# A neighbourhood-quantile layer: small writes behind the vector engine's operations, shorter sort operations, and a last pair finished batch by batch

## The chip, the cores and the metric

The kernel runs on one core of a Trainium2 chip. A core has five engines with a queue each: TensorE (PE in the profile, its weight loads PEld), VectorE (DVE), ScalarE (ACT), GpSimd (POOL) and SyncE (SP). The engines run their own instructions in order and wait for one another through semaphores. The metric is the time of one execution on the device in microseconds; lower is better.

## What is computed

For 16 graphs of 1024 nodes with 64 channels, every node aggregates its neighbours' features by quantiles and passes the result through a small two-layer network. The reference, cut to what matters:

```python
h = relu(layernorm(x))
neigh = (adj > 0) & ~eye
rank = cumsum(neigh) - neigh                    # place of a neighbour in its row
skip = where(nb > 10, (nb + 1) // 2, 1)         # nb: number of neighbours
rem = neigh & (skip > 1) & (rank % skip == skip - 1) & mask
nd = (adj with rem and rem.T dropped) > 0
s = sort(where(nd, h, inf), over the neighbours)        # per node and channel
agg = sum(w * quantile(s, tau) for tau, w in ((.25, .25), (.5, .5), (.75, .25)))
y = (relu((h + agg) @ W1 + b1) @ W2 + b2) * mask
return x + y
```

## The kernel before

The 16 graphs (batches) are worked in 8 pairs. For one batch, `prepare` does what precedes the sort: `load` turns the adjacency rows into signs and transposes them, `drop` (L979, tile `rem`) finds the edges that are dropped, `keep` and `order` sort the nodes by their number of neighbours (L1047, tile `perm`, is the one-hot matrix of that order), and `collect` writes for every node the list of its neighbours (tile `idx`). The features lie in a table in DRAM (`gtab`).

The sorted nodes form 8 tiles of 128, and the tiles form four classes of like degree: tile 0 with 13 slots, tiles 1 to 3 with 11, tiles 4 and 5 with 9, tiles 6 and 7 with 7. For each slot, tile and batch one indirect DMA on POOL's queue (`gather` in `fetch`, L1250) fetches the rows of 128 neighbours into a tile `g` (`g0`, `g1`, `g4`, `g6` by class): 126 gathers for a pair, 1008 in all. The 32 nodes of highest degree of each batch are finished apart, in groups of 8 batches (tiles `gg`, `fetch_group`, `aggregate_group`), and `scatter` (L1498) writes their rows of the output by two indirect DMAs for a group.

`sort` runs a fixed network over the slots of one class. A step of the network takes `n` comparisons of lines at once: one DVE operation writes the minima (L1288), one the maxima (L1289); steps that need one side alone are L1285. A line holds the class's tiles, both batches and 64 channels: 384 numbers in a partition for the 11-slot class, 256 for the 9- and 7-slot classes, 128 for the 13-slot class and the group. The operations are therefore up to 768 wide. At the end the slots are multiplied with the quantiles' weights (L1296) and added up by PE (L1298, one fp32 matmul with the identity for each slot). `let_go` puts a one-element write into a tile `pause` (L1268) behind an operation whenever some 0.8 us of sort operations have gone by without one; `arrange` keeps those writes as `tails` of their operation.

`aggregate` does this for both halves of a pair's tiles (half 0: classes 13 and 11; half 1: classes 9 and 7), both batches together, and `terms` (L1312, L1314) splits the sum into three bf16 terms, tile `o`. `mlp` then, for one batch and each 512 nodes, builds a one-hot matrix (`one_hot`, L1373, tile `at_p`), brings the nodes back into their order with it (L1392 `high`, L1397 `low`, 8 matmuls each), and applies the two layers (L1410, L1411, L1414, `output`).

The order of each engine's queue isn't the order of the code: `arrange` takes all instructions, gives each a cost (`Step.cost`), simulates five engines and fixes the order in which each engine runs its own. `settle` ties instructions into a run that must stay in order. The gathers stand in a queue of their own that `weave` empties at an even rate beside the other work. In the program's order the last steps are: aggregation of the last pair, its four one-hot matrices, `mlp` for batches 14 and 15, then the scatter of the last group and a check value (`worst`, `flag`), which decides whether a general version of the layer has to run.

Of the kernel before, what the change touches and what calls it, by code (L numbers as in the profile page):

```python
# [43 lines left out]
P = 128  # L44
N = 1024
C = 64
# [42 lines left out]
SPREAD = 160  # L89

# [510 lines left out]
class Step:  # L601
# [11 lines left out]
    def cost(self):  # L613
        sides = self.writes + self.reads
        most = max([u.count for u in sides] or [1])
        if self.engine == "PE":
            n, lines = self.writes[0].count, self.writes[0].lines
            if any(u.size == 4 for u in self.reads):
                busy = 223 if n <= 64 else max(428, n / 0.6)
            else:  # L620
                busy = max(25, n / 2.4 + 3)
            return busy * 1.15 / (4 if lines[1] - lines[0] <= 32 else 2 if lines[1] - lines[0] <= 64 else 1), 200
# [17 lines left out]
def arrange(tc, runs, tails=()):  # L640

    steps, found, number = [], {}, {}
    for ins in list(tc.nc.cur_bb.bb.instructions):
        if type(ins).__name__.startswith("BassTile"):
            continue
        if ins.name in tails:
            at = found[tails[ins.name]]
            at.tail.append(ins)
            number[ins.name] = len(number)
            at.busy += Step(ins, 0).busy  # L650
            found[ins.name] = at
            continue
        found[ins.name] = Step(ins, len(steps))
        steps.append(found[ins.name])
# [82 lines left out]

    for steps in sequence.values():
        alike = iter(sorted((i for s in steps for i in s.tail), key=lambda i: number[i.name]))
        line = [i for s in steps for i in (s.ins, *(next(alike) for _ in s.tail))]  # L740
# [8 lines left out]
def list_layer(  # L749
# [25 lines left out]
    def settle(run):  # L775

        runs.append([ins.ins.name for ins in run])
        for ins, then in zip(run, run[1:]):
# [6 lines left out]
            tc.info.no_tile_sem_insts.add(ins.ins.name)  # L785
        if len(run) > 1:
            tc.declare_fence(run[-1].ins, group=f"run{len(runs)}")

# [168 lines left out]
    def drop(b):  # L957
# [5 lines left out]
        for t in range(NT):  # L963
# [15 lines left out]
            nc.vector.tensor_scalar(rem[:, t], dist, 1.0, half[:, t:t + 1], OP.add, OP.is_equal)  # L979
# [32 lines left out]
    def order(b):  # L1012
# [30 lines left out]
        nc.vector.scalar_tensor_tensor(mask2[:, b], place_f, float(FEW), mask[:, b], OP.is_ge, OP.mult)  # L1043
        yield 1.2
        perm = wk.tile([P, NT, N], BF16, name="perm", tag="wide", bufs=1)
        for t in range(NT):
            nc.vector.tensor_scalar(perm[:, t], turned, place_f[:, t:t + 1], None, OP.is_equal)  # L1047
# [173 lines left out]
    tails = {}  # L1221
# [3 lines left out]

    queue = deque()
# [11 lines left out]
    def fetch(m, classes=CLASSES, halves=(0, 1)):  # L1238

        for tiles, slots in classes:  # L1240
# [8 lines left out]
            def gather(h, slot, k, at, tiles=tiles, lo=lo):  # L1249
                return nc.gpsimd.indirect_dma_start(  # L1250
                    out=gathered[m, tiles][:, slot, k - lo, h], out_offset=None, in_=tables[2 * m + h][0],
                    in_offset=bass.IndirectOffsetOnAxis(ap=lists[2 * m + h][:, at:at + 1], axis=0),
                    element_offset=tables[2 * m + h][1],
                )

# [7 lines left out]
    pause = cst.tile([P, 1], F32, name="pause")  # L1263

    def let_go(held, ins):
        if held < 0.8:
            return held
        tails[nc.vector.memset(pause, 0.0).ins.name] = ins.ins.name  # L1268
        return 0.0

    def sort(lines, plan, first, coef, acc):

        size = lines.shape[2]
        held = 0.0
# [5 lines left out]
        _, _, steps, ends, taken = plan  # L1280
        for n, a, da, b, db, f, df, back, what in steps:
            pa, pb = at(a, da, n), at(b, db, n)
            cost = 0.16 + n * size / 960
            if f < 0:
                ins = nc.vector.tensor_tensor(pa if back else pb, pa, pb, OP.min if what == "min" else OP.max)  # L1285
            else:
                one, other = (OP.min, OP.max) if what == "<" else (OP.max, OP.min)
                nc.vector.tensor_tensor(at(f, df, n), pa, pb, one)  # L1288
                ins = nc.vector.tensor_tensor(pa if back else pb, pa, pb, other)  # L1289
                cost *= 2  # L1290
            yield cost
            held = let_go(held + cost, ins)
        for n in taken:
            now, ends = ends[:n], ends[n:]
            v = at(now[0], now[1] - now[0] if n > 1 else 0, n).rearrange("p s (k c) -> p s k c", c=C)
            ins = nc.vector.tensor_tensor(v, v, coef(first, n)[:, :, :, None].to_broadcast(list(v.shape)), OP.mult)  # L1296
# [8 lines left out]
            held = let_go(held + cost, ins)  # L1305
# [23 lines left out]
    def aggregate(m, o):  # L1329
# [4 lines left out]
        for half in (0, 1) if last else (1, 0):  # L1334
            acc = psum.tile([P, 4, 2, C], F32, name="acc", tag="agg", bufs=2)
            parts = CLASSES[2 * half:2 * half + 2][::1 if last else -1]
            for tiles, slots in parts:
                lo, n = tiles[0], len(tiles)
                nc.tensor.matmul(
                    acc[:, lo - 4 * half:lo - 4 * half + n], ident32, gathered[m, tiles][:, slots - 1],  # L1340
                    start=((tiles, slots) == parts[0]), stop=False, skip_group_check=True,
                )
            line = {}
            for tiles, slots in parts:
                for k in tiles:
                    for s, slot in enumerate(PLANS[slots][1]):
                        line[k, s] = gathered[m, tiles][:, slot, k - tiles[0]]
                        if s >= FULL[k] and (k, s) not in HOSTS:
                            nc.vector.memset(line[k, s], BIG)
            for host, guest, first, stop in GUESTS:  # L1350
                if host in line:
                    nc.scalar.copy(line[guest][first:stop], line[host][first:stop])
            for host, lo, hi in BARE:
                if host in line:
                    nc.vector.memset(line[host][lo:hi], BIG)
            for tiles, slots in parts:
                lo, n = tiles[0], len(tiles)
                g = gathered.pop((m, tiles))
                plan = PLANS[slots]
                yield from sort(  # L1360
                    g.rearrange("p s n h c -> p s (n h c)"), plan, window(tiles, slots)[0],
                    lambda s, many: coef[:, s:s + many, lo:lo + n].rearrange("p s n h -> p s (n h)"),
                    acc[:, lo - 4 * half:lo - 4 * half + n],
                )
            if half and not last:
                fetch(m + 1, CLASSES[2:])
            terms(acc, [o[:, 4 * half:4 * half + 4, :, C * n:C * n + C] for n in range(3)])

    def one_hot(b, n, tag="at_p", bufs=1):

        at = wk.tile([P, NT, HALF], BF16, name="at_p", tag=tag, bufs=bufs)
        for t in range(NT):
            nc.vector.tensor_scalar(  # L1373
                at[:, t], iota[:, n * HALF:(n + 1) * HALF], node[:, b, t:t + 1], None, OP.is_equal
            )
            if t % 2:
                yield 0.6
# [4 lines left out]
    def mlp(b, o):  # L1382

        res = wk.tile([P, NT, C], F32, name="y")
        nc.sync.dma_start(out=res, in_=x[b].rearrange("(t p) c -> p t c", p=P))
        for n in range(2):
            if (b, n) not in placed:
                yield from one_hot(b, n)
            at = placed.pop((b, n))
            high = psum.tile([P, HALF], F32, name="high", tag="agg", bufs=2)  # L1390
            settle([
                nc.tensor.matmul(high, o[:, t, 0:2 * C], at[:, t], start=(t == 0), stop=(t == NT - 1))  # L1392
                for t in range(NT)
            ])
            low = psum.tile([P, HALF], F32, name="low", tag="agg", bufs=2)
            settle([
# [375 lines left out]
```

## Time and profile before

| what | value |
|---|---|
| median of 3 runs (lowest, highest) | 1578.8 us (1578.0 to 1582.2) |
| the profiled execution's own time | 1582.0 us |
| its span in the profile | 1580.2 us |
| DVE busy | 1191.0 us, 75% |
| PE busy | 1071.0 us, 68% |
| ACT busy | 917.2 us, 58% |
| operations at most 128x384 wide among L1288, L1289 on `g` | 288 of 816 |
| writes to `pause` (L1268) | 578, 59 ns each |
| 16 DMA engines, share of the span | 19.4% and 9.7% for the two dynamic queues |

A row of the page gives an engine, the operation's line and tiles, how often it ran, its busy time, the mean of one, and how long its engine stood idle before it and what ended that. A row of the timeline gives start, duration, engine, line and, in brackets, the idle time before. Times are microseconds from the start of the span.

### The profile page before, as it was taken

The page shows a single profiled execution, that of the slowest core. Times are in us where ns is not written, and L with a number is a line of the kernel's source. Part 1 is how long each engine was busy: PE and PEld are TensorE (multiplying, and loading weights), DVE is VectorE, ACT ScalarE, POOL GpSimd, SP SyncE. Part 2 cuts the span into 40 slices and gives each one's busy share as a digit, 9 for nine tenths or more (in the row PEclk, how much of TensorE's full clock was granted, in tenths as well). Part 3 has the DMA queues.
Part 4 walks back from the last instruction along what each step waited for, and adds up shares of the span by engine and source line. Part 5 has one row for each costly group of instructions (what it writes and reads, how often), then busy time and mean ns, then how long its engine had stood idle before and what let it go on. Part 6 is the DMA issues. An engine that isn't in the chain of part 4 may idle for free.

```text
span 1580.2 us, 25600 instructions
## 1 busy us (share of the span) xinstructions
PE 1071.0 (68%) x8385; PEld 664.2 (42%) x8385; DVE 1191.0 (75%) x3723; ACT 917.2 (58%) x2496; POOL 1137.8 (72%) x1051
## 2 busy tenths in 40 slices
PE   6777867889887887888569845588758822602235
PEld 3444544555554555455245534354535412301122
DVE  5615489865997789868884899977988897697660
ACT  6998886987958695978367841766825300200001
POOL 3277776777777777777777777777777777777730
PEclk9989979899998999899679976899888955855568
DMA  6453432442523252325122422222311211211100
GB/s 208 118 159 93 116 110 62 113 116 64 149 69 112 53 149 58 111 59 143 50 71 73 118 78 45 73 84 56 86 28 26 46 31 26 55 24 23 22 11 18
DMA packets 128481, 122.71 MB, mean 78 GB/s; under 512 B 94514, under 2 KB 95026, under 8 KB 128338
## 3 DMA queue, kind: packets, MB, share of 16 engines
q1 hardware_dynamic: 94994, 86.77, 19.4%
q0 software_dynamic: 33344, 34.21, 9.7%
q8 instruction: 68, 1.11, 0.3%
q14 instruction: 75, 0.61, 0.1%
HBM read 110.10 MB, written 9.07 MB: 75 GB/s over the span
## 4 chain that ended last, share of the span: by engine, by line
POOL 32%; ACT 20%; PE 14%; issue 14%; DVE 12%; DMA 6%; DVEq 0%; POOLq 0%; SPq 0%; ACTq 0%
POOL g L1250 31%; PE codeP L1072 5%; DMA g<-gtab,idx 4%; ACT dist L978 4%; ACT sg L891 3%; DVE g L1288 3%; ACT ne L911 3%; DVE g L1289 2%; ACT kept L1001 2%; ACT waste L1170 2%; ACT waste L1165 1%; ACT xt L1178 1%; PE acc L1298 1%; PE rk L968 1%; DMA xt<-in_x_dram 1%
## 5 line engine op out<-in xcount | busy, mean ns | idle before, releaser
L1250 POOL DMA_INDIRECT g<-gtab,idx x1008 | 1089.7, 1081 | 361.3 <-issue 288.0
L1288 DVE TENSOR_TENSOR g<-g 128x512 f32<-128x512 f32 (+3 forms) x408 | 280.7, 701 | 40.9 <-DMA g<-gtab,idx 25.9
L1289 DVE TENSOR_TENSOR g<-g 128x512 f32<-128x512 f32 (+3 forms) x408 | 281.4, 702 | 11.1 <-DMA gg<-g 8.4
L1298 PE MATMUL acc<-g,kf 128*128 128x256 f32 (+2 forms) x448 | 143.4, 461 | 176.5 <-DVE pause L1268 105.2
L1072 PE MATMUL codeP<-pack,perm 128*128 128x332 bf16 x1024 | 185.3, 323 | 21.4 <-DVE perm L1047 18.4
L978 ACT ACTIVATE dist<-rk,bias 128x512 f16<-128x512 f32 x256 | 168.4, 698 | 27.8 <-DVE bias L953 10.7
L1298 PEld LDWEIGHTS acc<-g,kf 128*128 128x128 f32 x448 | 89.5, 231 | 204.1 <-DVE pause L1268 111.4
L968 PE MATMUL rk<-kb,cnt 128*128 128x512 bf16 x256 | 113.2, 442 | 74.5 <-ACT dist L978 68.2
L1001 ACT ACTIVATE kept<-kp 128x512 fp8e4<-128x512 f32 x248 | 149.2, 617 | 14.0 <-PE kp L996 11.9
L898 PE MATMUL tp<-kb,sg 128*128 128x128 bf16 x1024 | 106.8, 243 | 69.3 <-ACT sg L891 52.6
L911 ACT ACTIVATE ne<-tp 128x512 fp8e4<-128x512 f32 x248 | 138.2, 608 | 19.4 <-PE tp L904 10.7
L973 PEld LDWEIGHTS <-ne 128*128 128x128 fp8e4 x1024 | 90.2, 109 | 133.1 <-issue 110.8
L1072 PEld LDWEIGHTS <-perm 128*128 128x128 bf16 x1024 | 93.9, 101 | 85.3 <-DVE perm L1047 43.9
L891 ACT ACTIVATE sg<-at 128x1024 bf16<-128x1024 f32 x121 | 126.6, 1076 | 2.4 <-DMA at<-in_adj_dram 2.3
L898 PEld LDWEIGHTS <-sg 128*128 128x128 bf16 x1024 | 81.2, 110 | 91.1 <-ACT sg L891 61.1
L973 PE MATMUL rk<-kw,ne 128*128 128x128 fp8e5 x1024 | 118.0, 243 | 0.0
L979 DVE TENSOR_SCALAR rem<-dist,half 128x1024 bf16<-128x1024 f16 x128 | 64.7, 506 | 61.7 <-ACT dist L978 60.7
L996 PE MATMUL kp<-kw,rem 128*128 128x128 fp8e5 x1024 | 99.7, 219 | 0.0
L991 PE MATMUL kp<-ne,kw 128*128 128x512 fp8e4 x256 | 98.5, 385 | 0.1
L992 PE MATMUL kp<-rem,kw 128*128 128x512 bf16 x256 | 97.6, 382 | 0.0
L1077 ACT CAST st<-codeP 128x4 bf16<-128x4 f32 x128 | 21.1, 165 | 119.6 <-PE codeP L1072 119.5
L1373 DVE TENSOR_SCALAR at_p<-iota,node 128x512 bf16<-128x512 f16 x256 | 82.8, 370 | 6.8 <-PE low L1397 6.7
(178 smaller groups left out, 2051.1 us busy)
## 6 DMA issues: line engine op xcount, KB each, us to landing
at<-in_adj_dram SPq DMA_DIRECT2D x122, 512.0 KB
g<-gtab,idx POOLq DMA_INDIRECT x1008
xt<-in_x_dram SPq DMA_DIRECT2D x16, 256.0 KB
y<-in_x_dram SPq DMA_DIRECT2D x16, 256.0 KB
gtab<-xt SPq DMA_DIRECT2D x16, 256.0 KB
out_dram<-y SPq DMA_DIRECT2D x16, 256.0 KB
spare<-in_adj_dram SPq DMA_DIRECT2D x6, 512.0 KB
gg<-g SPq DMA_DIRECT2D x32, 48.0 KB
```

The source lines that it names most:

```text
L891: nc.scalar.activation(sg, at, AF.Sign)
L898: run.append(nc.tensor.matmul(tp[:, s], sg[:, m * P:(m + 1) * P], ident16, start=(s == 0), stop=(s == 3 and t // 4 != n), skip_group_check ...
L911: nc.scalar.activation(to, tp, AF.Relu, saturate=False)
L968: run = [nc.tensor.matmul(rk, cnt[:, ts], blocks[:, 4 * n:4 * n + 4, None].to_broadcast([P, 4, P]), start=True, stop=False, skip_group_che ...
L973: run.append(nc.tensor.matmul(rk[:, s * P:(s + 1) * P], ne[:, 4 * n + s, ts], upper, start=False, stop=(s == 3), skip_group_check=True,))
L978: nc.scalar.activation(dist[:, n * HALF:(n + 1) * HALF], rk, AF.Abs, bias=bias[:, t:t + 1])
L1001: nc.scalar.activation(kept[:, 4 * n:4 * n + 4], kp, AF.Relu, saturate=False)
L1072: run.append(nc.tensor.matmul(flat, perm[:, t, k * P:(k + 1) * P], pack[:, t], start=False, stop=(t == NT - 1), skip_group_check=True,))
L1250: return nc.gpsimd.indirect_dma_start(out=gathered[m, tiles][:, slot, k - lo, h], out_offset=None, in_=tables[2 * m + h][0], in_offset=bas ...
L1288: nc.vector.tensor_tensor(at(f, df, n), pa, pb, one)
L1289: ins = nc.vector.tensor_tensor(pa if back else pb, pa, pb, other)
L1298: nc.tensor.matmul(acc, ident32, lines[:, s], start=False, stop=(s == now[-1] and not ends), skip_group_check=True)
```

## The change

It has seven parts.

1. A helper `opened` puts a one-element write into `pause` (64 elements of bf16 in turn) behind every operation of `sort`, and behind those that make `rem`, `perm` and `at_p`. `let_go` is gone. In `arrange` such a write counts 12 ns on its operation.
2. With `PART = 384`, `sort` cuts every operation into parts of at most 384 numbers in a partition: a 768-wide one into two of 384 (for weights of the 9- and 7-slot classes three of 256), a 512-wide one into two of 256.
3. All operations of a step form one run (`settle`), which the planner keeps together and which has one point that others wait for. Within the run, an operation that reads the lines which the one before it has read no longer waits for it (`declare_no_dep`), when another instruction stands between the two.
4. Each gather counts up a semaphore `issued` when POOL has issued it, and the gather with the number k in POOL's order (k from 2) waits until k-1 of them have been issued.
5. For the last pair, half 1 is worked by batch: gathers of classes 9 and 7 for batch 14, then for batch 15; sort, sum, `terms` and `mlp` for batch 14, then for batch 15. The one-hot matrices and the matmuls over tiles 0 to 3 (`sums`, `late`) of a batch stand before the sort of that batch's half 1. `mlp` adds `high` and `low` on DVE, uses one W1 matmul instead of two, takes its bias matmul ahead, and writes each 512 rows of the output when they are done.
6. The last group's scatter moves ahead of the last pair's aggregation and takes 96 rows; the 32 rows of the last pair are put into `o` by `bring_back`, and `mask2` of these two batches is the plain mask. The check value is computed there as well.
7. The planner's cost of an fp32 matmul is `60 + n` ns below 512 columns and 850 at 512, before 223 or `n / 0.6`.

```diff
+PART = 384
...
             if any(u.size == 4 for u in self.reads):
-                busy = 223 if n <= 64 else max(428, n / 0.6)
+                busy = 60 + n if n < 512 else 850
...
-def arrange(tc, runs, tails=()):
+def arrange(tc, runs, loose, tails, paced):
...
+            found[ins.name].busy += 12
+            gaps.setdefault(tails[ins.name], []).append(ins)
...
+        if s.engine == "DVE" and ins.name in joined:
+            at = found[ins.name] = found[joined[ins.name]]
             at.tail.append(ins)
...
+    for k, s in enumerate(s for s in sequence["POOL"] if s.ins.name in paced[1]):
+        if k > 1:
+            paced[1][s.ins.name].wait_op(paced[0], k - 1, "sem-ge")
...
+        for ins in line:
+            if ins.name in loose and at[loose[ins.name]] < at[ins.name] - 1:
+                tc.declare_no_dep(ins, loose[ins.name], reason="read in order by one engine")
...
-            tc.info.no_tile_sem_insts.add(ins.ins.name)
+            if "PE" in str(ins.ins.engine):
+                tc.info.no_tile_sem_insts.add(ins.ins.name)
...
+    pause = cst.tile([P, 64], BF16, name="pause")
+
+    def opened(ins):
+
+        at = len(tails) % 64
+        tails[nc.vector.memset(pause[:, at:at + 1], 0.0).ins.name] = ins.ins.name
+        return ins
...
-            nc.vector.tensor_scalar(rem[:, t], dist, 1.0, half[:, t:t + 1], OP.add, OP.is_equal)
+            opened(nc.vector.tensor_scalar(rem[:, t], dist, 1.0, half[:, t:t + 1], OP.add, OP.is_equal))
...
-            nc.vector.tensor_scalar(perm[:, t], turned, place_f[:, t:t + 1], None, OP.is_equal)
+            opened(nc.vector.tensor_scalar(perm[:, t], turned, place_f[:, t:t + 1], None, OP.is_equal))
...
-                    element_offset=tables[2 * m + h][1],
+                    element_offset=tables[2 * m + h][1], engine_sem=issued,
...
-    def let_go(held, ins):
-        if held < 0.8:
-            return held
-        tails[nc.vector.memset(pause, 0.0).ins.name] = ins.ins.name
-        return 0.0
...
+        most = max(1, PART // size)
+
+        def parts(n):
+            return [(k, min(most, n - k)) for k in range(0, n, most)]
...
+            for k, many in parts(n):
+                pa, pb = at(a + k * da, da, many), at(b + k * db, db, many)
...
+                    run.append(opened(
+                        nc.vector.tensor_tensor(at(f + k * df, df, many), pa, pb, OP.min if what == "<" else OP.max)
+                    ))
+            for k, many in parts(n) if f >= 0 else ():
...
+                others.append(opened(
+                    nc.vector.tensor_tensor(pa if back else pb, pa, pb, OP.max if what == "<" else OP.min)
+                ))
+            loose.update((then.ins.name, ins.ins.name) for ins, then in zip(run, others))
...
+                settle(run + others)
...
+            for sides in ((0, 1), (1, 2)) if last and half else ((0, 2),):
+                hs, one = slice(*sides), sides[0] if last and half else None
...
+                if last and not half:
+                    bring_back(m, o)
+                if one is not None:
+                    yield from between(one, True)
...
+            def between(h, done):
+                b = 2 * m + h
+                if not done:
+                    for n in range(2):
+                        yield from one_hot(b, n, *((("at_p", 1), ("ne", 2)), (("ne", 2), ("wide", 1)))[h][n])
+                    begun[h] = [sums(o[:, :, h], placed[b, n], n, range(NT // 2), late=True) for n in range(2)]
+                else:
+                    yield from mlp(b, o[:, :, h], begun[h])
+
             yield from aggregate_group(grp - 1)
-            yield from sums
...
+            scatter(grp - 1, P - 2 * SLICE)
+            yield from aggregate(m, o, between)
```

## The prediction

> **What bounds the kernel now.** I read the page's busy table and slices first, then the costly groups, POOL's waits, and POOL's and DVE's timelines side by side. The slices show POOL at the same level from the second slice to the last but one:
>
> ```profile
> POOL 3277776777777777777777777777777777777730
> ```
>
> ```profile
> L1250 POOL DMA_INDIRECT g<-gtab,idx x1008 | 1089.7, 1081 | 361.3 <-issue 288.0
> L1288 DVE TENSOR_TENSOR g<-g 128x512 f32<-128x512 f32 (+3 forms) x408 | 280.7, 701 | 40.9 <-DMA g<-gtab,idx 25.9
> L1298 PE MATMUL acc<-g,kf 128*128 128x256 f32 (+2 forms) x448 | 143.4, 461 | 176.5 <-DVE pause L1268 105.2
> ```
>
> ```profile
> POOL g L1250 <- issue: 288.0, 945, 0.3
> POOL g L1250 <- DVE idx L1116: 55.0, 3, 46.0
> POOL g L1250 <- DMA g<-gtab,idx: 7.9, 26, 0.3
> ```
>
> A level of 7 looks like slack and isn't. A gather is followed by 0.30 us of "issue" 945 times, and the longest wait for a landing is also 0.3: between 68.3 (the first gather) and 1517.5 POOL never waits for data except once early (55 us, mostly before the first gather). DVE and PE wait for gathers, not the reverse. So POOL sets the end of the gathers, and 63 us of tail follow. The shortest gather is 0.94 us (the view of tile `g`: 940 minimum, 952 median), the mean 1.081: 1008 x 0.141 = 142 us are lost inside gathers. Where:
>
> ```profile
> 1447.04 1.55 POOL L1250 DMA_INDIRECT g<-gtab,idx  x1 [0.30 <-issue]
> 1448.90 1.68 POOL L1250 DMA_INDIRECT g<-gtab,idx  x1 [0.30 <-issue]
> 1456.06 1.27 POOL L1250 DMA_INDIRECT g<-gtab,idx  x1 [0.30 <-issue]
> 1482.96 0.94 POOL L1250 DMA_INDIRECT g<-gtab,idx  x1 [0.30 <-DMA g<-gtab,idx]
> ```
>
> ```profile
> 1448.81 0.96 DVE L1289 TENSOR_TENSOR g<-g 128x768 f32<-128x768 f32 x1
> 1449.71 0.06 DVE L1268 MEMSET pause<- 128x1 f32 x1
> 1455.96 0.56 DVE L1285 TENSOR_TENSOR g<-g 128x384 f32<-128x384 f32 x1
> 1456.44 0.95 DVE L1288 TENSOR_TENSOR g<-g 128x768 f32<-128x768 f32 x1
> ```
>
> With DVE idle (1482.96) a gather takes 0.94. The one at 1448.90 ends at 1450.58, 0.81 after the DVE operation beside it ended (1449.77); the one at 1456.06 ends 0.81 after 1456.52, where L1285 ends and L1288 follows with no write between. So a gather needs something of DVE's about 0.13 us after its start, waits for the end of the running operation, then takes 0.81. Length of the operations is what costs; a `pause` write is not needed at such a boundary. Beside 768-wide pairs the gathers lock to every second operation (1.99 us apart).
>
> **What the Trainium skill says.** "SBUF — State Buffer", section "Who interferes with whom": a DVE instruction with two SBUF inputs contends with a GpSimd instruction that reads SBUF, and the loser blocks until the other instruction has ended. The trace agrees (1.68 against 0.94). The same section infers that `tensor_tensor` would not hold up descriptor generation; here it does, and the measurement decides. "DMA: Bandwidth & Descriptors", section "SWDGE vs HWDGE vs iDMA": descriptors of POOL's DMAs are computed by GpSimd's cores, which fits a gather that occupies POOL though its data lands later.
>
> **Shorter operations (parts 1 to 3).** For an operation of pitch L the time lost to gathers arriving at random is (L - 0.13)^2 / 2, summed over operations and divided by the 1448 us of gathering. Pitches are start to start in DVE's timeline: 768 wide 0.877, 512 0.611, 384 0.477, 256 0.344, `rem` and `perm` 0.395, `at_p` 0.263; counts are from the groups kept apart by shape. Before: 320 x 0.279 + 272 x 0.116 + 346 x 0.060 + 222 x 0.023 + 21 for the rest (`rem`, `perm`, `at_p`, and the `cand` operations of L1095) = 168 us squared; / 1448 x 1008 = 117 us, where 142 were measured (locking makes the rest, a factor 1.21). After: 576 of 384 and 640 of 256 replace the wide ones: 576 x 0.060 + 640 x 0.023 + 47 = 96; / 1390 x 1008 x 1.21 = 84. Gain **58 us**. Beside 768-wide pairs a locked gather would go from 1.99 to 3 x 0.48 = 1.44. From below I take 40 (using full durations in place of pitches), from above 80 (writes opening boundaries that are closed today: behind `perm`, run back to back, single gathers take up to 1.68).
>
> On DVE itself each added part costs 0.08 us (2 x 0.477 - 0.877): 288 for the 768-wide pairs and singles with their weights, 64 more for weights in three parts, 272 for the 512-wide, together 624 x 0.08 = 50 us. The writes go from 578 to some 2330, but the pitch with one between is the same within 0.002 us: 4 us. From 200 to 1440 DVE is busy 1028 of 1240 us; idle time that ends on gathers is 42 there, on ACT and PE about 150. After, 1075 of 1190. POOL stays the later engine, but DVE's margin of 42 is used up; I charge **+8** (0 to 45). The runs keep others out for up to four operations (2 us); behind them wait PE's sums and `keep`'s and `collect`'s DVE work, which have such idle time today.
>
> **Pacing (part 4).** It adds one wait and one count to each of 1008 gathers. What is queued behind a waiting gather is every later gather. The wait is for the gather before the previous one, which ended at least 0.3 + 0.94 us earlier, and semaphore waits in front of gathers already occur (26 for landings, with 0.30 like all others), so they are read while the previous gather runs. I take **0**. No row shows a gather with such a count: bounds -20 (the 0.30 shrinks) and +30 us (0.03 each). Arranging costs (part 7) change order alone: 0, within the range.
>
> **The tail (parts 5, 6).** The chain of waits shows it:
>
> ```profile
> 1516.60 2.54 DMA g<-gtab,idx
> ...
> 1530.68 0.99 DVE g L1296 x2
> 1531.70 4.36 PE acc L1298 x12
> 1536.08 0.59 ACT o L1312
> ...
> 1563.00 2.88 DMA out_dram<-y
> ...
> 1566.86 1.00 POOL out_dram L1498
> ```
>
> From the start of the last gather to the last output's issue: 46.4 us. After, for one batch: landing 2.6; the 7-slot sort with 7 paired steps of 2 x 0.34 + 0.12 for the dependent next step, the single ones 0.9, weights 1.0, together 7.5 (12.4 now); fp32 sums at half the width 3.0 (5.4 now); `terms` at half the width 1.7 (2.7 now); then one `mlp` of which tiles 0 to 3 are done: sums 1.4, copy 0.6, addition 0.7, W1 1.1, ReLU 0.7, W2 0.9, two DVE operations 0.9, and 1.4 for the second 512 nodes behind it, 7.7 (24 now for four halves in line). Sum 22.5, saved **24**. Batch 14's sort, 9-slot and 7-slot, needs some 19 us of DVE and lies beside batch 15's 24 gathers (24 x 1.33 = 32 us), and so does its `mlp`; without that cover 10 us come back. I charge +2 for the slip.
>
> Behind the last output today: its landing, two scatters in sequence (the second waits 3.2 us for the first), the end at 1580.2, 17.2 us. The closing after the last scatter alone takes 1572.06 to 1580.2 = 8.1; with scatter and check value ahead, that is what remains: saved **9**. The moved scatter's two DMAs now stand among the last pair's gathers: 2 x 1.3 and one 0.9 wait as at 1142.46, **+3.5**; they also wait for the outputs of batches 12 and 13 on SP's queue, issued by 1374.5, long before the group's rows are ready (1454), and gathers behind them would wait if the planner put them too early: up to +10 in the range. `bring_back` needs the group's sum only and lies beside gathers.
>
> **Sum.** Against the profiled execution's span of 1580.2 (1582.0 as timed): -58 + 8 + 0 - 24 + 2 - 9 + 3.5 = -77.5, span 1502.7. The median shown is 1578.8, 1.4 below that span, so I predict **1501**.
>
> **Rivals.**
> (a) DVE takes over. For it: 83% busy from 200 to 1440, 50 us more work, and 150 us of idle time on ACT and PE that needn't shrink. Against: those waits do shrink when DVE runs late. Of the 58 about 15 remain, tail as above: 1501 + 35 = **1536**.
> (b) The writes open more than the ends of operations do, and the excess falls to 40 of 142: 1501 - 44 = **1457**. For it: `perm`'s long gathers. Against: boundaries between sort operations already let gathers in.
> (c) On the other side: the count of part 4 costs POOL time on each gather, or arrives so late that the 0.30 grows. It decides from 78 / 1008 = 0.077 us a gather; at 0.15 it costs 151 us: **1651**. Against: waits are read ahead.
> (d) Nothing comes of the gathers and the tail is eaten by a new order: about **1579**.
>
> **Chances.** Forecast 0.67, (a) 0.13, (b) 0.10, (c) 0.08, (d) 0.02. Range 1455 to 1545: it holds (a), (b) and the bounds above. What is told from no change is 0.3%, some 5 us: faster 0.90, same 0.02, slower 0.08.
>
> **What would show it.** Gathers' mean near 1.02 with the gap still 0.30; beside 768-wide steps a cadence near 1.4; DVE busy some 50 us more; last gather near 1463; some 31 us from it to the end and no scatter there. Wrong if the gap between gathers isn't 0.30, if gathers wait for DVE (`idx` or a free `g`), or if the mean of a gather stays at 1.08.

## The result, and the profile after

| | before | after |
|---|---|---|
| median of 4 runs (lowest, highest) | 1578.4 us (1577.0 to 1582.2) | 1559.9 us (1557.7 to 1562.8) |
| span of the profiled execution | 1580.2 us | 1561.1 us |
| first gather, last gather start | 68.3, 1516.6 us | 69.0, 1525.8 us |
| from the start of the last gather to the end | 63.6 us | 35.3 us |
| DVE busy | 1191.0 us | 1245.4 us |
| excess: time over 0.94 us in all of POOL's indirect DMAs | 146.1 us | 127.0 us |

The ratio is 0.988 (0.9856 to 0.9904): 1.2% faster, where 4.9% was forecast. In ten of the runs below, each marked so, the kernel before itself took 2.58 to 2.62 ms (medians); every version of the changed kernel was 3.4 to 4.6% slower than it there, for a reason that no run shows, and the argument rests on none of these times.

The table already holds the surprise. The tail (from the start of the last gather to the end) lost 28 us, near the 31 forecast, but the gathers end 9 us *later* than before. The page of the changed kernel (slices, then the costly groups; L1277 is the gather, L1320 and L1325 the minima and maxima, L810 the write):

```profile
DVE  4625399964898789878997499989799899889784
...
POOL 3177777577777777777777777777477777788771
...
L1277 POOL DMA_INDIRECT g<-gtab,idx x1008 | 1071.0, 1062 | 372.5 <-DMA g<-gtab,idx 300.9
L1320 DVE TENSOR_TENSOR g<-g 128x256 f32<-128x256 f32 (+1 forms) x675 | 308.0, 483 | 10.7 <-issue 5.6
...
L810 DVE MEMSET pause<- 128x1 bf16 x2340 | 138.1, 59 | 0.0
```

The mean of a gather fell to 1.062 only. POOL's slices show a 5 early on, a dip to 4 past two thirds and two digits of 8 near the end, where nearly every digit before was 7. POOL's waits name the dips:

```profile
POOL g L1277 <- DMA g<-gtab,idx: 300.9, 974, 0.8
POOL g L1277 <- DVE idx L1143: 46.7, 1, 46.7
POOL out_dram L1623 <- DMA out_dram<-y: 18.1, 1, 18.1
POOL g L1277 <- issue: 16.9, 7, 14.3
```

The 5 is the wait of 14.3 us in the last line. The profile names no releaser for it, but the gather behind it starts at 290.7, right after a list that DVE writes at 289.7; before, that list came at 275.1 and the wait was 8.7 us. The third line is the scatter of the *first* group. It stands where it stood before, behind 756 gathers. What has changed are the times; first before, then after, each time the output that it follows as SP issues it, and the scatter's first DMA:

```profile
1104.51 0.38 SPq L1419 DMA_DIRECT2D out_dram<-y  x1
1138.99 1.29 POOL L1498 DMA_INDIRECT out_dram<-gx,gto  x1 [0.31 <-issue]
```

```profile
1127.68 0.39 SPq L1516 DMA_DIRECT2D out_dram<-y  x1
1131.21 1.05 POOL L1623 DMA_INDIRECT out_dram<-gx,gto  x1 [18.08 <-DMA out_dram<-y]
```

POOL comes to this place 26 us earlier than before (1113.1 and not 1138.7), the output comes 23 us later, and 18.1 us of gathers wait behind the scatter. The digits of 8 hold this, in POOL's timeline and in DVE's:

```profile
1389.46 0.98 POOL L1277 DMA_INDIRECT g<-gtab,idx  x1 [0.30 <-DMA g<-gtab,idx]
1390.75 28.92 POOL L1277 DMA_INDIRECT g<-gtab,idx  x1 [0.30 <-DMA g<-gtab,idx]
1419.97 0.95 POOL L1277 DMA_INDIRECT g<-gtab,idx  x1 [0.30 <-DMA g<-gtab,idx]
```

```profile
1417.96 0.54 DVE L1339 TENSOR_TENSOR g<-g,coef 128x384 f32<-128x384 f32 x1
1417.97 0.06 DVE L810 MEMSET pause<- 128x1 bf16 x1
1418.44 0.41 DVE L1325 TENSOR_TENSOR gg<-gg 128x256 f32<-128x256 f32 x1
1418.45 0.40 DVE L810 MEMSET pause<- 128x1 bf16 x2
1418.88 0.56 DVE L1320 TENSOR_TENSOR gg<-gg 128x384 f32<-128x384 f32 x1
```

One gather takes 28.92 us. From 1390.91 on DVE starts each operation before the one ahead has ended (1418.44 before 1417.96 + 0.54), through 64 ends with writes behind them. The operation at 1418.88 is the first that starts only after the one ahead (1418.44 + 0.41 = 1418.85) is over (a stall), since it reads that one's result. The gather ends at 1419.67, 0.82 after that stall began. A second one takes 5.38 us at 1506.05.

The chain of waits of the last stage:

```profile
1506.05 6.86 DMA g<-gtab,idx
...
1515.89 2.95 PE acc L1344 x12
...
1539.74 2.94 PE acc L1344 x12
...
1551.92 1.90 PE yp L1530 x16
```

It leaves POOL at its second long gather, 20 us before the last one, and goes on through DVE's sort and PE's sums of batch 14 and then of batch 15. So POOL led up to there. How far behind it the DVE stood, this doesn't show; that took experiments.

### The profile page after: what moved, and what is told of

It reads as the page before. It is cut to its first block, busy times and chain, and to the rows that moved or that the text cites. A ratio compares the mean times of both kernels' runs of the same rounds, so it can differ in the third digit from the quotient of the medians.

```text
span 1561.1 us, 29017 instructions
## 1 busy us (share of the span) xinstructions
PE 1084.3 (69%) x8411; PEld 672.8 (43%) x8411; DVE 1245.4 (80%) x6125; ACT 911.0 (58%) x2504; POOL 1118.7 (72%) x1051
## 4 chain that ended last, share of the span: by engine, by line
ACT 25%; PE 25%; POOL 18%; issue 17%; DVE 10%; DMA 4%; POOLq 0%; DVEq 0%; SPq 0%; ACTq 0%
POOL g L1277 17%; PE codeP L1099 7%; ACT dist L1002 5%; PE acc L1344 4%; ACT sg L915 4%; ACT ne L935 3%; ACT kept L1025 3%; DVE g L1320 2%; ACT waste L1192 2%; ACT waste L1197 2%; DMA g<-gtab,idx 2%; PE tp L922 2%; PE high L1460 1%; DMA xt<-in_x_dram 1%; DVE found L1131 1%
## 5 line engine op out<-in xcount | busy, mean ns | idle before, releaser
L1277 POOL DMA_INDIRECT g<-gtab,idx x1008 | 1071.0, 1062 | 372.5 <-DMA g<-gtab,idx 300.9
L1320 DVE TENSOR_TENSOR g<-g 128x256 f32<-128x256 f32 (+1 forms) x675 | 308.0, 483 | 10.7 <-issue 5.6
L1325 DVE TENSOR_TENSOR g<-g 128x256 f32<-128x256 f32 (+1 forms) x675 | 308.1, 484 | 5.6 <-DMA gg<-g 5.6
L1344 PE MATMUL acc<-g,kf 128*128 128x128 f32 (+2 forms) x472 | 135.8, 436 | 140.7 <-DVE g L1339 138.8
L1099 PE MATMUL codeP<-pack,perm 128*128 128x332 bf16 x1024 | 197.1, 341 | 17.9 <-DVE perm L1074 17.8
L992 PE MATMUL rk<-kb,cnt 128*128 128x512 bf16 x256 | 109.5, 428 | 65.3 <-ACT dist L1002 58.3
L1099 PEld LDWEIGHTS <-perm 128*128 128x128 bf16 x1024 | 100.9, 107 | 90.5 <-DVE perm L1074 33.9
L810 DVE MEMSET pause<- 128x1 bf16 x2340 | 138.1, 59 | 0.0
```

The source lines that it names most:

```text
L810: tails[nc.vector.memset(pause[:, at:at + 1], 0.0).ins.name] = ins.ins.name
L1099: run.append(nc.tensor.matmul(flat, perm[:, t, k * P:(k + 1) * P], pack[:, t], start=False, stop=(t == NT - 1), skip_group_check=True,))
L1277: ins = nc.gpsimd.indirect_dma_start(out=gathered[m, tiles][:, slot, k - lo, h], out_offset=None, in_=tables[2 * m + h][0], in_offset=bass ...
L1320: nc.vector.tensor_tensor(at(f + k * df, df, many), pa, pb, OP.min if what == "<" else OP.max)
L1325: nc.vector.tensor_tensor(pa if back else pb, pa, pb, OP.max if what == "<" else OP.min)
L1344: nc.tensor.matmul(acc, ident32, lines[:, s], start=False, stop=(s == now[-1] and not ends), skip_group_check=True)
```

## The experiments

T1: POOL sets the end, and the long gathers and the scatter's wait took the gain back. T2: the DVE, with 54 us more work, stands right behind and sets the end as soon as POOL is ahead. T3: pacing costs. All kernels below start from the changed one and compute everything. A change of the source also shifts the order that the planner picks for some instructions.

**The same kernel again.** Is the long gather an accident?

> The changed kernel once more, nothing edited. If a gather that misses its turn waits until the DVE stalls, and the order of instructions decides where: long gathers come back, one of over 10 us and together 15 to 40 us, time 1555 to 1565. If the 28.92 us gather was an accident: no gather over 4 us, the last gather starts some 30 us earlier (near 1495), and the end comes no more than 10 us earlier, since the DVE stands close behind. The 18 us wait of the first group's scatter comes back within 5 us in either case.

1558.0 us, ratio 0.9837 (0.9786 to 0.9888). POOL's timeline and, after the dots, its waits:

```profile
1392.28 28.11 POOL L1277 DMA_INDIRECT g<-gtab,idx  x1 [0.30 <-DMA g<-gtab,idx]
...
POOL out_dram L1623 <- DMA out_dram<-y: 16.3, 1, 16.3
```

The long gather comes back at its place (and the second with 5.38 us), as does the scatter's wait. They belong to this program and aren't the accident of one execution.

**A stall in each exchange.**

```diff
-            if ins.name in loose and at[loose[ins.name]] < at[ins.name] - 1:
+            if False and at[loose[ins.name]] < at[ins.name] - 1:
```

> The kernel of the run a3 again, where kernels, the one before the change among them, take 1.58 ms and not 2.6: the maxima wait for the DVE operations that they follow again. T1 (gathers held by unbroken runs): each exchange again has a stall of the DVE, in which a waiting gather gets its turn: no gather over 3 us, the 32 us of the two long ones come back, the time falls from 1560 to 1528 to 1540; the mean of the gathers falls from 1.06 to near 1.03. T2 (the DVE with its extra work became the late engine): a wait more per exchange makes the DVE still later, the time stays at 1560 or rises by up to 15. T3 (pacing costs): no change, 1557 to 1563.

1570.5 us, ratio 0.9924 (0.9896 to 0.9952). The view of tile `g` on POOL (shortest/median/longest in ns, first to last start):

```profile
L1277 POOL DMA_INDIRECT g<-gtab,idx x1008: 938/947/1705, 69.2 to 1499.8; - x168
```

The mechanism of T1 held: no gather over 1.71 us, and the last one 26.0 us earlier. Its time didn't: the end came 6 us *later*, 67.5 us behind the last gather. DVE's busy time rose to 1261.1 us, 15.7 more. So T2 holds as well.

**The first group's scatter behind the last gathers.**

```diff
+            scatter(0)
             scatter(grp - 1, P - 2 * SLICE)
...
-            if ("out", grp) in gathered and m == 2 * grp + 6:
+            if ("out", grp) in gathered and False:
```

> The first group's scatter is issued beside the second group's, behind the last gathers, so it no longer stands among gathers in the GpSimd queue; everything else is as in the changed kernel and everything is computed. If GpSimd alone sets the end: the 18.1 us for which the queue waited for the output DMA go, less 1.5 to 3 us for the scatter's issue at the end, and the time falls by 12 to 17 us to 1543 to 1549. If the DVE with the split operations is the second limit right behind (as the runs with the waits kept and with early splitting have it: gathers over at 1500 and 1488, end at 1567 and 1569), the gathers end some 15 us earlier, the end moves by no more than 6 us (1553 to 1566). Long gathers may come and go with the changed timing in either case (+-15 us for the gathers' end).

1555.9 us, ratio 0.9852 (0.982 to 0.9884); span 1554.5. Tile `g` on POOL, then DVE's busy time by windows (start:end, length, busy; granted clock, DMA share and GB/s follow):

```profile
L1277 POOL DMA_INDIRECT g<-gtab,idx x1008: 938/947/1709, 69.1 to 1473.6; - x168
```

```profile
1400.00:1450.00 50.00, 49.51 (x230) 0.50 0.14 25
1450.00:1500.00 50.00, 43.85 (x194) 0.59 0.08 16
1500.00:1550.00 50.00, 32.95 (x170) 0.85 0.05 12
```

and all that the DVE waited for from 1390 to 1560, bar one wait of 1.6 us (total, times, longest):

```profile
DVE yp L1534 <- PE yp L1530: 8.7, 5, 5.8
DVE highs L1487 <- PE low L1466: 7.0, 1, 7.0
DVE few L1618 <- ACT o L1616: 2.8, 1, 2.8
```

This is the run that decides. The scatter's wait is gone and, with the new timing, so are the long gathers, though no wait was put back. The gathers end 52 us earlier, and the end moves by 6.6 (medians: 4.0). Over the first of these windows the DVE is full, and no gather is among what it waits for. Had POOL still set the end, the span would have been some 1473.6 + 35.3 = 1509 (an estimate, with the tail of the changed kernel); it is 1554.5, as T2 has it.

**Operations whole again**, the rest of the change left: `PART = 768`.

> The splitting undone alone (operations up to 768 elements wide again), with writes, runs, pacing, the last pair by batch and the moved scatter left; in a run by itself. The DVE loses some 600 operations and as many writes, 45 to 50 us of work. If GpSimd alone sets the end: the gathers' excess over 0.94 us rises from 127 us by 40 to 60, the last gather starts 20 to 40 us later than 1526, the time is 1580 to 1600. If the DVE sets it or stands right behind (T2): the time falls below the changed kernel's, to 1530 to 1555, and the excess stays under 160 us. DVE busy falls from 1245 to near 1200 in both.

1551.3 us, ratio 0.9802 (0.9771 to 0.9833): without its second part the change is better. Page, then tile `g` on POOL, then tile `idx` (the neighbour lists; at the end of the row's times stands the start of the last list):

```profile
L1277 POOL DMA_INDIRECT g<-gtab,idx x1008 | 1086.1, 1078 | 367.6 <-DMA g<-gtab,idx 300.2
```

```profile
L1277 POOL DMA_INDIRECT g<-gtab,idx x1008: 938/947/4384, 69.1 to 1518.4; - x168
```

```profile
L1143 DVE SCALAR_TENSOR_TENSOR idx<-bit,low x17: 165/256/332, 68.6 to 1230.2; 128x104 int32<-128x104 f32 x15, 128x24 int32<-128x24 f32 x1, 128x80 int32<-128x80 f32 x1
```

Against the run before it: the excess of POOL's indirect DMAs is 142.3 us and not 97.9, so splitting is worth 44 us of gathers. For that the DVE is busy 1245.4 us and not 1203.4, and the last list starts at 1260.6 and not at 1230.2. Of the 42 us of added work 30 came through to the lists, though the DVE has some 257 us of idle time before 1150 in both. Most of that time ends on ACT and PE, whose own waits end on the DVE in part (PE `codeP` on DVE `rest` and `perm`); that this circle passes the delay on is read from the waits, no run cuts it. The granted clock isn't the difference (0.842 here, 0.841 there). The scatter, at its old place, waits 0.31 us: its output is issued at 1093.1, so the wait of 18.1 us came with the split operations. With whole operations POOL sets the end, 33.0 us behind the last gather's start. That last gather starts 1.8 us later than before: the 29 us gained on the kernel before are the tail's.

**Split only where POOL was thought to be late** (the first five pairs), with the waits kept and the scatter late:

```diff
-        most = max(1, PART // size)
+        most = max(1, widest[0] // size)
...
+        widest[0] = PART if m < pairs - 3 else 768
```

> Operations split to 384 only in the aggregations of the first five pairs (until some 1100 us, where GpSimd sets the pace and the DVE has 250 us idle), whole again from the sixth pair on, where the DVE is full; the maxima wait for the DVE again; the first group's scatter behind the last gathers. Everything is computed. If the account of the first runs holds (splitting is worth some 37 us of gathers before 1150 us and nothing after, the stalls prevent long gathers, the scatter's wait is gone): the last gather starts 30 to 40 us earlier than with whole operations (1518), near 1480 to 1488, no gather over 3 us, and the end follows within 40 to 60 us of it: 1520 to 1540. If the DVE sets the end whatever the gathers do (T2 in its strong form): 1545 to 1555, as with whole operations, with the gathers ending 50 us or more before the end.

1566.2 us, ratio 0.9888 (0.9867 to 0.991).

```profile
L1277 POOL DMA_INDIRECT g<-gtab,idx x1008: 939/947/1712, 70.2 to 1488.1; - x168
```

A miss in time, outside both expectations: the gathers end as hoped and the end comes 80.6 us behind the last one. The last list starts at 1264.5, 34 us later than with whole operations. The kept waits account for little of that (1264.7 with them and 1261.1 without, both split throughout), so the early splitting cost about 30 us, by this estimate: the early stages had no room on the DVE. Why the whole operations of the last three pairs won none of it back stays open.

**Split at 512**, scatter late: half-way between the two engines (`PART = 512`).

> Operations split at 512 elements instead of 384 (768 becomes 512 and 256, 512 stays whole), and the first group's scatter behind the last gathers; everything is computed. If the DVE's added work holds the end (T2): splitting at 384 cost the DVE 43 us, at 512 it costs some 12 to 20, so the DVE busy time falls from 1245 to 1215 to 1225, the stages move up by 10 to 25 us, and with the last gather starting at 1485 to 1505 the time is 1530 to 1545, below the 1551 of whole operations and the 1556 of this scatter with 384. If something else holds the end at 1555, the time stays within 5 us of 1556.

1540.7 us, ratio 0.9717 (0.969 to 0.9743), the fastest of all. Tile `g` on POOL and tile `idx`:

```profile
L1277 POOL DMA_INDIRECT g<-gtab,idx x1008: 938/978/5371, 68.9 to 1489.8; - x168
```

```profile
L1143 DVE SCALAR_TENSOR_TENSOR idx<-bit,low x17: 166/255/283, 68.4 to 1238.8; 128x104 int32<-128x104 f32 x15, 128x24 int32<-128x24 f32 x1, 128x80 int32<-128x80 f32 x1
```

DVE busy 1225.2 us, 20.2 less than with 384; the lists 21.8 us earlier; the end 15.4 us earlier than the same kernel with 384 (spans 1539.1 and 1554.5), though the gathers end 16.2 us *later*. With its added work the DVE held the end: gathers that end later go with an earlier end, so the sign alone shows it.

**Whole operations without any write.**

```diff
-PART = 384
+PART = 768
...
-        at = len(tails) % 64
-        tails[nc.vector.memset(pause[:, at:at + 1], 0.0).ins.name] = ins.ins.name
```

> Whole operations (up to 768 wide) without any write behind them, once more; everything is computed. To be held against whole operations with writes (1551 us, gathers' excess 142 us, longest gather 4.4 us). If a boundary between two DVE operations lets a waiting gather in without a write: excess within 20 us of 142 and time within 10 us of 1551 (1541 to 1561), longest gather under 6 us. If the write is what opens: many gathers over 3 us, excess over 200 us, the last gather starts 50 us later or more, time over 1600.

1570.5 us, ratio 0.9929 (0.9902 to 0.9956), between the two expectations: 19 us slower than with the writes, but excess (160.7 and not 142.3) and longest gather (5.87 us) as for boundaries that open without a write. In its POOL and DVE timelines:

```profile
591.66 4.13 POOL L1275 DMA_INDIRECT g<-gtab,idx  x1 [0.30 <-DMA g<-gtab,idx]
```

```profile
592.49 1.55 DVE L1323 TENSOR_TENSOR g<-g 128x512 f32<-128x512 f32 x2
593.96 0.42 DVE L1314 TENSOR_TENSOR g<-g 128x256 f32<-128x256 f32 x1
594.29 0.69 DVE L1318 TENSOR_TENSOR g<-g 128x512 f32<-128x512 f32 x1
595.01 0.69 DVE L1323 TENSOR_TENSOR g<-g 128x512 f32<-128x512 f32 x1
```

The gather ends at 595.79, 0.81 after the first end at which the DVE stalled (594.98; the next starts at 595.01), having passed the ends before it. Such misses are rare. Count a gather as meeting an operation when a TENSOR_TENSOR (the two-input operations of the sort) runs 0.13 us after its start, and as a miss when it ends over 0.3 us later than 0.81 after that operation's end. Then 547 of 559 gathers are let in at the end of the operation, with no write anywhere; 12 miss and lose 23.4 us. With writes (the run with whole operations) 3 of 535 miss, for 6.1 us. The difference of 17.3 us is most of the 18.4 us of excess. Whether the writes let those gathers in, or other timing and order do, isn't shown: moving one scatter did away with long gathers too, its writes unchanged.

The same count over all runs of the changed kernel and its versions, those at 2.6 ms left out, gives 22 misses. Eleven ended at a stall of the DVE and 8 where something else than a TENSOR_TENSOR (`rem`, a MAX8, a MEMSET into `g`) came next; nearly all the ends that they passed were followed at once by another TENSOR_TENSOR.

**Pacing taken out.** Only runs where the kernel before took 2.6 ms tell of it.

```diff
-        if k > 1:
+        if False:
             paced[1][s.ins.name].wait_op(paced[0], k - 1, "sem-ge")
...
-                    element_offset=tables[2 * m + h][1], engine_sem=issued,
+                    element_offset=tables[2 * m + h][1],
```

> The count of gathers issued and the wait for it are taken out; the order is the same. T1 and T2: the wait lies in the 0.305 us between two gathers that were there before, so the gap stays at 0.305 and the time within 3 us of the changed kernel, apart from long gathers that the slightly different timing makes or unmakes (+-20 us). T3 (pacing costs): the gap falls by 0.02 us or more for each of some 1050 instructions, the time falls by over 20 us with no change in the long gathers.

2708.3 us, where the unedited kernel took 2721.8 beside it; all four executions lie below its four. The median idle time between two gathers is 0.305 us in both traces, as it is before the change and after it. So no cost on the gathers themselves is visible; the effect on the kernel's time where it takes 1.56 ms stays untried.

A second pair for pacing, with whole operations:

> Whole operations (up to 768 wide) with writes, and the count of gathers with its wait taken out; everything is computed. To be held against whole operations with pacing (1551 us, gap between gathers 0.305 us, last gather from 1518 us), where GpSimd sets the end. If pacing is free: the gap stays at 0.305 us, the last gather starts within 8 us of 1518 and the time is 1543 to 1559. If pacing costs: the gap falls by 0.02 us or more, for some 1000 gathers 20 us or more, time under 1535.

2695.3 us (before 2588.7) without pacing; with it 2709.4 (before 2616.3). Held against the kernel before, the one without pacing is now the slower (1.043 and 1.037). The gap is 0.305 us in both again. Inconclusive in time.

**The other runs where the kernel before took 2.6 ms.** Beside pacing taken out (before 2619.3 us), the same kernel, the waits kept and the scatter late:

> The changed kernel once more, nothing edited, to see what of its profile comes back. T1 (gathers held by unbroken runs): a gather is granted at a boundary between two DVE operations or misses it by its timing, and where the DVE then runs without a stall it goes on missing; the order of instructions is fixed, so one or two gathers of over 4 us should be seen again, near 1390 us or elsewhere, together some 15 to 40 us, and the time is 1557 to 1563. If the 28.92 us gather was an accident of one execution, no gather takes over 3 us and the profiled execution is some 30 us shorter (near 1530). The 18 us wait of the first group's scatter for its output DMA should come back within 3 us in either case, since it follows from the order alone.

2721.8 us.

> The maxima wait for the DVE operations that they follow again (the declared absence of a dependency inside an exchange run is taken back); nothing else is edited. T1: each exchange again has a stall of the DVE, in which a waiting gather gets its turn: no gather over 3 us, the 32 us of the two long ones come back as time, the time falls by 20 to 32 us to 1528 to 1540; the mean of the gathers falls from 1.06 to near 1.03. T2 (the DVE with its extra work became the late engine): a wait more per exchange makes the DVE still later, the time stays at 1560 or rises by up to 15. T3 (pacing): no change, 1557 to 1563.

2739.3 us.

> The first group's scatter is issued beside the second group's, behind the last gathers, so it no longer stands among gathers in the GpSimd queue; everything is computed. T1: the 18.1 us for which the queue waited for the output DMA go, the tail grows by the scatter's own issue (some 1.5 to 3 us), so the time falls by 12 to 17 us to 1543 to 1548, if the long gathers stay as they are (they may move, since the times of the gathers against the DVE change: +-20 us). T2: gathers then only wait elsewhere for the DVE, no more than 5 us are gained. T3: no change beyond 3 us.

2713.6 us. With the kernel before at 2616.3 us, the same kernel, the scatter late, both edits at once, and whole operations:

> The changed kernel once more, nothing edited, to see what of its profile comes back. T1 (a gather that misses its turn waits until the DVE stalls): the order of instructions is fixed, so long gathers come back at the same places, one of over 10 us and together 15 to 40 us, and the time is 1557 to 1565. If the 28.92 us gather was an accident of one execution, no gather takes over 3 us and the execution is some 10 us shorter at most, since the DVE stands close behind. The 18 us wait of the first group's scatter comes back within 3 us in either case.

2726.9 us.

> The first group's scatter is issued beside the second group's, behind the last gathers, so it no longer stands among gathers in the GpSimd queue; everything is computed. If GpSimd alone sets the end: the 18.1 us for which the queue waited for the output DMA go, less 1.5 to 3 us for the scatter's issue at the end, the time falls by 12 to 17 us to 1543 to 1549. If the DVE is the second limit right behind it (T2, as the run with the waits kept has it, where the gathers ended 26 us earlier and the end came 6 us later): the gathers end some 15 us earlier, the end moves by no more than 6 us (1553 to 1563). Long gathers may come and go with the changed timing in either case (+-15 us for the gathers' end).

2707.6 us.

> Both: the maxima wait for the DVE again, and the first group's scatter stands behind the last gathers; everything is computed. If GpSimd sets the end: 20 us less than with the waits kept alone, 1547 to 1553. If the DVE sets it (T2): the last gather starts near 1480, 20 us earlier than with the waits kept alone (1500), and the end stays within 4 us of 1570.

2728.0 us.

> The splitting undone alone (operations up to 768 elements wide again), with writes, runs, pacing, the last pair by batch and the moved scatter left. The DVE loses some 600 operations, 50 us of work. If GpSimd sets the end: the gathers' excess over 0.94 us rises from 127 us by 40 to 60, without the long gathers by 60 to 80, the last gather starts 20 to 40 us later, the time is 1580 to 1600, above before less the tail. If the DVE sets it (T2): the time falls below the changed kernel's, to 1530 to 1555, however long the gathers are. DVE busy falls from 1245 to near 1195 in both.

2709.4 us. And whole operations without writes (before 2578.5 us):

> Whole operations (up to 768 wide) without any write behind them; runs, pacing, the last pair by batch and the moved scatter are left, everything is computed. To be held against the run with whole operations and writes (1551 us, gathers' excess 142 us, longest gather 4.4 us). If a boundary between two DVE operations lets a waiting gather in without a write: excess and time stay within 10 us of those (1541 to 1561), longest gather under 6 us. If the write is what opens: inside a run without stalls gathers wait for several operations, many gathers over 3 us, excess over 200 us, the last gather starts 50 us later or more, time over 1600.

2684.7 us. No expectation is decided by any of these times: only 100 to 138 of the 1042 indirect DMAs meet a TENSOR_TENSOR here (592 in the changed kernel at 1.56 ms), and no long gather comes back in the same kernel. The edits stand above with times near 1.56 ms, but for pacing and for the waits kept with the scatter late.

## Why the prediction was wrong

**POOL bounds the kernel, a gather waits for the end of the running operation and then takes 0.81.** Right for the kernel before, and the waiting still so for 590 of the 592 gathers of the changed kernel that meet a TENSOR_TENSOR. That it is the making of descriptors that waits isn't shown: a gather also reads its list `idx`, and no run separates the two.

**Shorter operations, 58 us (40 to 80).** Nearly right: the excess fell from 146.1 to 127.0, and without the two long gathers (28.0 and 4.4 over 0.94) to 94.6, a gain of 51.5. Against whole operations within the changed kernel it is 44. DVE's added work came to 54.4 us where 50 + 4 was forecast, but this is luck: the splitting cost 42.0 (1245.4 against 1203.4) and not 50, all else 12.4 (1203.4 against 1191.0) and not 4.

**"POOL stays the later engine, but DVE's margin of 42 is used up; I charge +8 (0 to 45)."** This is the step that failed. With the gathers freed, the end came at 1554.5 where POOL's path would have given about 1509: 45 us, the upper end of the bound, where 8 was taken. The idle time was read as room, with DVE's waits for ACT and PE expected to shrink. From 200 to 1440 us the margin did go, as forecast: the waits that end on gathers (those on ACT's copies of gathered rows with them) fell from 42.2 to 4.8 us. The other waits for ACT and PE, which were to shrink, went from 140.8 to 154.0, and 42 us of added work brought the lists 30 us later. Rival (a), "DVE takes over", was right in kind at 1536 and too small.

**The runs "keep others out for up to four operations".** A second step failed here. The price was looked for in what the DVE keeps from PE and ACT, and nothing was charged to POOL. It lay there: runs without a stall held one gather for 28.92 us (two sorts woven together) and another for 5.38, which put 32.4 us on POOL's path. "A `pause` write is not needed at such a boundary" was nearly right (547 of 559), and the few exceptions were the costly ones.

**The moved scatter, +3.5, up to +10 if put too early.** The last group's scatter ended up behind the gathers and cost them nothing. The danger that was named, a scatter that waits for outputs, came true for the first group's, which wasn't moved: a faster POOL reached it before the outputs, now later, were there, and 18.1 us of the DVE's delay fell on POOL's path.

**The tail, -24, +2 and -9.** Right in sum: 63.6 to 35.3 us, 28.3 saved where 31 was forecast.

**Pacing, 0.** The gap of 0.305 us stands with and without it; what it does to the time of the kernel is untried.

The sum of the changed kernel: the last gather was forecast near 1463 (1516.6 - 58 + 3.5 = 1462.1) and started at 1525.8, 63.7 later. Of these, 32.4 are the two long gathers, 6.5 the smaller gain, 13.7 scatters (17.2 against the 3.5 charged), 5.6 the early wait for a list (14.3 and not 8.7 us; a wait for `idx` was named as a sign of being wrong), 5.0 ten short waits, and 0.7 a later first gather; together 63.9. The tail was 2.7 longer than forecast, and the 8 charged for the DVE didn't come as a term of its own: 63.7 + 2.7 - 8 = 58.4, the miss in span. It would be wrong, though, to call the long gathers and the scatter the cause of 50 lost microseconds: taken away, they give 6.6, because the DVE stands behind.

What makes a gather miss a boundary isn't settled. The waits kept removed all long ones, but so did the changed timing and order with the scatter late. The long misses end at a stall or at an operation of another kind; what starts them stays open.

## What to carry to other kernels

An idle time of 20% on an in-order engine was no room for more work here, where its waits ended on engines that wait for it in turn: look at when its results are ready, and ask what the end would be if the bounding engine were free. When a cost is moved from one engine to a second, try the steps between: here 512 (span 1539.1) beat both 384 (1554.5) and 768 (1551.4). A wait in an in-order queue that costs nothing today can cost once the queue runs faster and the work that it waits for runs slower, though nobody has moved it: here the first group's scatter.

## What was not expected of the hardware

- A GpSimd gather can be passed over at many ends of DVE operations, writes between them or not: 28.92 and 28.11 us through 64 and 62 ends, until the DVE stalled.
- Without any write, 98% of the gathers (547 of 559) were still let in at the first end.
- A count and a semaphore wait on each of about 1000 gathers left the 0.305 us between two of them unchanged.
